# A tokenizer, attention and mixture-of-experts tower in float32: the second MLP product from seven products of quarters, with small work moved between engines

## Chip, cores and metric

The kernel runs on one core of one Trainium2 chip, in float32 throughout. The metric is the device time of one execution in microseconds. Where a profile is read, it is one profiled execution. Engines are named as the profile names them: PE is TensorE (PEld its weight loads), DVE is VectorE, ACT is ScalarE, POOL is GpSimd, SP is SyncE, which issues most DMAs.

## The reference, cut to what matters

The input x is (4, 64, 512, 64): 4 x 4096 = 16384 tokens of 256 features come out.

```python
h = tok(x)                       # patches of 16 at stride 8, real FFT, product with W: (tokens, 256)
x = layernorm(h)
a = layernorm(x) * g1 + b1
q, k, v = a @ Wq.T + bq, a @ Wk.T + bk, a @ Wv.T + bv
mem_t = decay * mem_(t-1) + k_t * v_t          # a scan along the tokens
x = x + q * mem
a = layernorm(x) * g2 + b2
x = x + relu(a @ W1.T + b1) @ W2.T + b2        # W1: 256 to 1024, W2: 1024 to 256, the second MLP product
h = h + x
t = layernorm(h)
p = softmax(t @ router.T)                      # 8 experts; two largest kept, scaled to sum 1
out = h + t + sum over the two experts e of p_e * (gelu(t @ w1[e]) @ w2[e] + b2[e])
```

## The kernel before, in words

**Blocks and stages.** The tokens are worked on in 32 blocks of 512 (`Block`, four tiles of 128 rows). The loop over the blocks (lines 973 to 1047) is a pipeline of three: in one turn `new` (block i) is embedded, normalised and taken through q, k, v and the scan; `mid` (i-1) goes through the MLP; `old` (i-2) is stored, its experts are chosen, and its rows are scattered to a table in DRAM, `xbuf`, sorted by expert. A `Tile` is 256 rows of one expert, read back from `xbuf`; four tiles per block go through the expert's two products in slots between the other work (`expert_step`, line 939, through `slot`, line 959), and their results are added to `out` by indirect DMAs of POOL (line 853).

**Order.** On PE, DVE, ACT and SP the order of the instructions is the order in which the program emits them (`manual_schedule`, line 970); each engine works through its queue in order. Only POOL's order is chosen by the scheduler. A turn of the loop emits: `embed` with an expert slot after it; eight `mlp_in` (first MLP product, line 482 applies ReLU on ACT into `aT`) with a second slot among them; the `logits` of `old` (line 553); `retention(0)`, `choose` of `old`, `retention(1)` (q, k, v products, line 298; ACT makes `ks`, DVE `kv`, the scan and `ret`); `place` (line 619) and `take` (line 696); a third slot; `mlp_out(0)`; `residual` (PE transposes of `ret`, line 451); a fourth slot; `mlp_out(1)`.

**What the change touches.**
- `mlp_out` (line 484): for two tiles of 128 rows at a time, 2 x 8 products of 128x128 by 128x256 into one `tm` buffer of PSUM; DVE adds it to `h` (line 499) and takes the mean and variance of the rows (lines 223, 224). After the second call the factor `rstd` is made on POOL (lines 243, 248), and DVE writes `tok`, the normalised rows.
- PSUM has four buffers `mm`, three `tm`, and a single one named `sm` (line 93). `sm` holds the logits, and then the counts of the placement.
- `embed` (to line 396): at its end DVE writes `zz` and `z`, two normalisations of `h`, four instructions each (line 252), with `rstd` from POOL. `zz` goes by ACT copies and a transposing DMA (line 286) to `hT`, which the q, k, v products read; `z` is needed at `residual`.
- `differences` (line 315): nine DVE operations on the next block's input.
- `choose` (line 565): thirteen small DVE operations on the logits, and one power on POOL. `place` (line 619): two products into `sm`, then DVE operations that read it (lines 629, 630) and give the row addresses; `weights` (line 599).
- `scatter` (line 642): POOL writes the rows of `old` to `xbuf`, two indirect DMAs for each of four tiles.
- `take` (line 696): small DVE operations on one partition that work out, for the next four tiles, the rows and the expert; SP reads that `table` in front of the tiles' loads (lines 775, 779).
- `Tile.sums` (line 838): DVE works out the weights of a tile's rows (`tile_share`, lines 842, 845) and multiplies the tile's results with them.

## Time and profile before

| | us |
|---|---|
| median of 3 runs | 2169.24 (2166.68 to 2170.31) |
| the profiled execution, its own time | 2168.11 |
| its span on the core | 2166.3 |
| a steady period (q, k, v products of one block to those of the next) | 63.4 |
| of this, DVE busy (993.30 to 1056.70) | 50.4 |
| of this, ACT busy | 25.9 |
| of this, POOL busy | 27.8 |

The groups of the page give one row for each line, engine and shape; each float32 matmul of the program stands there as two instructions.

```profile
L492 PE MATMUL tm<-w_sb,aT 128*128 128x256 f32 x2048 | 453.5, 380 | 1.7 <-DVE h L499 1.7
L492 PEld LDWEIGHTS tm<-w_sb,aT 128*128 128x128 f32 x2048 | 389.3, 190 | 55.1 <-DVE h L499 2.1
L597 POOL TENSOR_TENSOR ex<-euler,second 128x4 f32<-128x4 f32 x32 | 34.6, 1080 | 236.7 <-DVE second L589 236.7
```

The number after the bar is the time in which at least one of the group ran, then the mean of one in ns, then the idle time of the engine just before. A mean of 380 ns with 2048 instructions in 453.5 us tells that they overlap: the time that one costs is that from start to start. The last row shows a group whose engine waits for another one most of the time.

### The profile page before, as it was taken

Reading aid. Unit: us, or ns where it says so; the run is one execution under the profiler, and the core shown is the slowest. Engines: PE = TensorE matmul, PEld = TensorE weight load, DVE = VectorE, ACT = ScalarE, POOL = GpSimd, SP = SyncE. Lnnn points to the kernel's source line nnn. Section 1 sums busy time; section 2 is a strip of 40 time slices with the busy share of each in tenths; the row PEclk is TensorE's granted clock in tenths of the full one; section 3 lists DMA queues with packets and bytes.
Section 4 is the critical chain, followed back from the end, with each engine's and each line's share of the span. In section 5 each row is a group of like instructions: output and inputs, shape, how many; then the busy total and the mean of one; then the engine's idle time right before and its main releaser. Section 6 shows DMA issues by size and latency. Waiting matters only on the chain.

```text
span 2166.3 us, 28918 instructions
## 1 busy us (share of the span) xinstructions
PE 2142.5 (99%) x8548; PEld 1545.3 (71%) x8548; DVE 1646.8 (76%) x5150; ACT 833.4 (38%) x1329; POOL 874.0 (40%) x760
## 2 busy tenths in 40 slices
PE   8999999999999999999999999999999999998999
PEld 6666666677776667776667777666777766676776
DVE  6678877787878778787777877877787787767454
ACT  1222333443334444333444433344443334442543
POOL 0022233444444344444334444443444444355444
PEclk9999999999999999999999999999999999999999
DMA  3032255765756675665777556577666657678753
GB/s 138 20 99 77 77 130 127 162 124 128 155 130 148 152 163 117 135 154 127 150 152 156 123 138 146 131 151 154 135 137 145 143 132 153 136 175 216 114 69 44
DMA packets 425389, 284.95 MB, mean 132 GB/s; under 512 B 355216, under 2 KB 391056, under 8 KB 421136
## 3 DMA queue, kind: packets, MB, share of 16 engines
q1 hardware_dynamic: 374304, 210.21, 41.1%
q0 software_dynamic: 49632, 67.39, 17.8%
q10 hardware_dynamic: 1296, 5.52, 0.8%
q8 instruction: 67, 1.10, 0.2%
q14 instruction: 90, 0.74, 0.1%
HBM read 118.36 MB, written 88.39 MB: 95 GB/s over the span
## 4 chain that ended last, share of the span: by engine, by line
PE 96%; DVE 2%; issue 1%; DMA 0%; another core or an unknown queue 0%; ACT 0%; POOL 0%; DVEq 0%; SPq 0%; POOLq 0%; ACTq 0%
PE mm L298 35%; PE tm L492 20%; PE tm L353 13%; PE mm L813 10%; PE tm L830 10%; PE sm L557 2%; PE tm L905 1%; PE tm L451 1%; PE mm L888 1%; PE mm L131 1%; PE mm L265 1%; PE sm L624 0%; PE sm L204 0%; DVE ks L426 0%
## 5 line engine op out<-in xcount | busy, mean ns | idle before, releaser
L853 POOL DMA_INDIRECT out<-y,xg x262 | 429.0, 1637 | 463.4 <-DVE y L849 221.0
L298 PE MATMUL mm<-hT,w_sb 128*128 128x512 f32 x1024 | 453.1, 595 | 3.5 <-issue 2.7
L492 PE MATMUL tm<-w_sb,aT 128*128 128x256 f32 x2048 | 453.5, 380 | 1.7 <-DVE h L499 1.7
L492 PEld LDWEIGHTS tm<-w_sb,aT 128*128 128x128 f32 x2048 | 389.3, 190 | 55.1 <-DVE h L499 2.1
L298 PEld LDWEIGHTS mm<-hT,w_sb 128*128 128x128 f32 x1024 | 195.1, 191 | 221.8 <-issue 207.4
L647 POOL DMA_INDIRECT xbuf<-row,to x248 | 243.5, 982 | 258.7 <-DVE full L708 182.3
L298 PE MATMUL mm<-hT,wqkv_sb 128*128 128x512 f32 x768 | 338.7, 597 | 0.0
L353 PE MATMUL tm<-wu,xv 128*128 128x256 f32 x1280 | 284.3, 381 | 0.0
L353 PEld LDWEIGHTS tm<-wu,xv 128*128 128x128 f32 x1280 | 244.4, 191 | 32.7
L821 ACT ACTIVATE ge<-mm,w 128x256 f32<-128x256 f32 x262 | 109.4, 470 | 404.9 <-issue 363.5
L298 PEld LDWEIGHTS mm<-hT,wqkv_sb 128*128 128x128 f32 x768 | 144.3, 191 | 169.0 <-issue 155.3
L813 PE MATMUL mm<-xT,w 128*128 128x256 f32 x1048 | 250.3, 382 | 1.4 <-DVE tile_share L842 1.4
L830 PE MATMUL tm<-w,ge 128*128 128x256 f32 x1048 | 247.7, 379 | 0.9 <-ACT ge L821 0.9
L482 ACT ACTIVATE aT<-mm,vec 128x512 f32<-128x512 f32 x256 | 172.4, 683 | 187.7 <-PE mm L298 187.0
L813 PEld LDWEIGHTS mm<-xT,w 128*128 128x128 f32 x1048 | 195.0, 191 | 38.1 <-issue 15.6
L830 PEld LDWEIGHTS tm<-w,ge 128*128 128x128 f32 x1048 | 199.4, 190 | 31.0 <-issue 3.3
L806 ACT COPY xT<-xh 128x512 uint16<-128x512 uint16 x262 | 181.6, 763 | 20.3 <-DMA xh<-xbuf 20.2
L243 POOL TENSOR_SCALAR rstd<-mv 128x4 f32<-128x4 f32 x62 | 41.6, 672 | 316.7 <-DVE mv L224 314.8
L278 ACT COPY planes<-zz 128x1024 uint16<-128x1024 uint16 x100 | 99.6, 1043 | 167.4 <-issue 86.8
L847 DVE TENSOR_TENSOR y<-tm,w 128x512 f32<-128x512 f32 x131 | 90.6, 692 | 70.8 <-PE tm L830 70.8
L416 ACT ACTIVATE ks<-mm,vec 128x512 f32<-128x512 f32 x64 | 44.0, 687 | 236.1 <-PE mm L298 236.1
L597 POOL TENSOR_TENSOR ex<-euler,second 128x4 f32<-128x4 f32 x32 | 34.6, 1080 | 236.7 <-DVE second L589 236.7
(155 smaller groups left out, 2443.0 us busy)
## 6 DMA issues: line engine op xcount, KB each, us to landing
w<-in_wex SPq DMA_DIRECT2D x113, 641.5 KB
xb<-in_x SPq DMA_DIRECT2D x32, 1040.0 KB
out<-h SPq DMA_DIRECT2D x31, 512.0 KB
bank<-in_wex ACTq DMA_DIRECT2D x8, 641.5 KB
out<-y,xg POOLq DMA_INDIRECT x262
xbuf<-row,to POOLq DMA_INDIRECT x248
xh<-xbuf SPq DMA_TRANSPOSE x131
xg<-xbuf SPq DMA_DIRECT2D x131, 4.0 KB
```

What stands on the lines that cost most here:

```text
L278: nc.scalar.copy(planes[:, :, i * D : (i + 1) * D], half)
L298: nc.tensor.matmul(ps, lhsT=w[:, k, ts(m, P)], rhs=rhs[:, k, :], start=k == 0, stop=k == KD - 1)
L353: nc.tensor.matmul(ps[:, n, :], lhsT=xv[:, i, j, :], rhs=wu[:, i, j, :], start=j == 0, stop=j == J - 1)
L482: nc.scalar.activation(self.aT[:, m, :], ps, AF.Relu, bias=vec[:, MB1 + m : MB1 + m + 1])
L492: last_product[0] = nc.tensor.matmul(ps[:, i, :], lhsT=self.aT[:, k, ts(u * 2 + i, P)], rhs=w2_sb[:, k, :], start=k == 0, stop=k == KH - 1,)
L647: write = nc.gpsimd.indirect_dma_start(out=xbuf, out_offset=bass.IndirectOffsetOnAxis(ap=self.to[:, c, t : t + 1], axis=0), in_=self.row[: ...
L806: nc.scalar.copy(halves[:, :, :, 1 - i], self.xh[:, i * KD : (i + 1) * KD, :])
L813: nc.tensor.matmul(ps[:, m, :], lhsT=self.w[:, k * D + m * P : k * D + (m + 1) * P], rhs=self.xT[:, k, :], start=k == 0, stop=k == KD - 1,)
L821: nc.scalar.activation(self.ge[:, m, :], ps[:, m, :], AF.Gelu, bias=self.w[:, 5 * D + m : 5 * D + m + 1])
L830: last_product[0] = nc.tensor.matmul(ps[:, c, :], lhsT=self.ge[:, k, ts(c, P)], rhs=w[:, (2 + k) * D : (3 + k) * D], start=k == 0, stop=k ...
L847: nc.vector.tensor_tensor(y, ps, w[:, 4 * D : 5 * D].unsqueeze(1).to_broadcast([P, 2, D]), ALU.add)
L853: add = nc.gpsimd.indirect_dma_start(out=out, out_offset=bass.IndirectOffsetOnAxis(ap=self.xg[:, c, NUMBER - D : NUMBER - D + 1], axis=0), ...
```

## The change

Of `take` the diff shows the lines after the change alone; before, each was on DVE (lines 715 to 744).

**Second MLP product.** `aT` is cut into four quarters (features by rows), `W2` into four (features by outputs), and the product of 2 x 2 quarters is made from seven products of quarters instead of eight, in Winograd's form of Strassen's scheme. `combine_weights` makes the three further combinations of weights once. `combine1` makes three combinations of `aT` on DVE, ahead of the q, k, v products of `new`; `combine2` the fourth, after `mlp_out(0)`. Each product of quarters is eight matmuls of 128x128 by 128x128. They stand in three calls: `mlp_out(0)`, one product, into the buffer `sm`; `mlp_out(1)`, two, into a `tm`, right after it; `mlp_out(2)`, four, where the second call was, two into the same `sm` and two into a `tm`. A copy on ACT and eight adds on DVE bring the seven into `h`.

**Choice of experts.** `choose` is emitted ahead of `retention(0)`, not between the two halves.

**`z`.** It is written by ACT (`result1`), four instructions between the two `ks` of the retention, with a small operation `less` on DVE after the first half of the retention.

**Weights of a tile's rows.** `tile_share` is worked out by POOL when the tile is turned, two tiles ahead, in three operations; in the last blocks by DVE as before. **The table** of `take` is worked out by POOL, from `base` on, in 17 operations that POOL has, except for the last blocks. **Differences**: one operation goes ahead of `zz`, the other eight stay. Some buffers are fewer (`xh` four instead of six). The scatters of the second and third tile now follow `mlp_out(0)` and `mlp_out(1)`.

```diff
@@ weights of the second product @@
-    w2_sb = const.tile([P, KH, D], F32)
-    nc.sync.dma_start(out=w2_sb, in_=w2.rearrange("(k p) d -> p k d", p=P))
+    w2_sb = const.tile([P, 7, KQ, P], F32)
+    w2_raw = w2.rearrange("(r k p) (c d) -> p r c k d", p=P, k=KQ, d=P)
+    for i, (r, c) in {B11: (0, 0), B21: (1, 0), B22: (1, 1), T1: (0, 1)}.items():
+        nc.sync.dma_start(out=w2_sb[:, i], in_=w2_raw[:, r, c])
+    def combine_weights():
+        nc.vector.tensor_tensor(w2_sb[:, T3], w2_sb[:, B22], w2_sb[:, T1], ALU.subtract)
+        nc.vector.tensor_tensor(w2_sb[:, T1], w2_sb[:, T1], w2_sb[:, B11], ALU.subtract)
+        nc.vector.tensor_tensor(w2_sb[:, T2], w2_sb[:, B22], w2_sb[:, T1], ALU.subtract)
+        nc.vector.tensor_tensor(w2_sb[:, T4], w2_sb[:, B21], w2_sb[:, T2], ALU.subtract)
...
@@ Block.differences, Block.embed @@
-        def differences(self, xb):
+        def differences(self, xb, part):
+            if part:
+                self.rest()
+                return
...
-            self.z = one.tile([P, TT, D], F32, name="z")
             self.zz = one.tile([P, TT, D], F32, name="zz")
             norm.apply(self.zz, self.h, 1)
-            norm.apply(self.z, self.h, 0)
+            self.norm1 = norm
+        def result1(self):
+            mean, rstd = self.norm1.mv[:, :, 0], self.norm1.rstd[:, 0, :]
+            less = small.tile([P, TT], F32, name="less")
+            self.z = one.tile([P, TT, D], F32, name="z")
+            nc.vector.scalar_tensor_tensor(less, mean, -1.0, rstd, ALU.mult, ALU.mult)
+            for t in range(TT):
+                nc.scalar.activation(
+                    self.z[:, t, :],
+                    self.h[:, t, :],
+                    AF.Identity,
+                    bias=less[:, t : t + 1],
+                    scale=rstd[:, t : t + 1],
+                )
...
@@ Block.combine1, combine2, mlp_out @@
             ps = feature_mm(w1_sb, self.hT, m)
             nc.scalar.activation(self.aT[:, m, :], ps, AF.Relu, bias=vec[:, MB1 + m : MB1 + m + 1])
 
+        def combine1(self):
+            self.A11, self.A12 = [self.aT[:, i * KQ : (i + 1) * KQ, : BLK // 2] for i in range(2)]
+            self.A21, self.A22 = [self.aT[:, i * KQ : (i + 1) * KQ, BLK // 2 :] for i in range(2)]
+            shape = [P, KQ, BLK // 2]
+            self.S1 = one.tile(shape, F32, name="tok")
+            self.S2 = one.tile(shape, F32, name="tokT")
+            self.S3 = self.A21
+            nc.vector.tensor_tensor(self.S1, self.A21, self.A22, ALU.add)
+            nc.vector.tensor_tensor(self.S2, self.S1, self.A11, ALU.subtract)
+            nc.vector.tensor_tensor(self.S3, self.A11, self.A21, ALU.subtract)
+        def combine2(self, place):
+            self.S4 = one.tile([P, KQ, BLK // 2], F32, name=place)
+            nc.vector.tensor_tensor(self.S4, self.A12, self.S2, ALU.subtract)
         def mlp_out(self, u, between=None):
+            def product(to, a, b):
+                for i in range(2):
+                    for k in range(KQ):
+                        last_product[0] = nc.tensor.matmul(
+                            to[:, i, :],
+                            lhsT=a[:, k, ts(i, P)],
+                            rhs=w2_sb[:, b, k, :],
+                            start=k == 0,
+                            stop=k == KQ - 1,
+                        )
+            def add(to, what):
+                nc.vector.tensor_tensor(to, to, what, ALU.add)
+            h = self.h.rearrange("p (a i) (c d) -> p a c i d", i=2, d=P)
+            U = self.aT[:, 0, : BLK // 2].rearrange("p (i d) -> p i d", d=P)
             if u == 0:
-                self.norm = Norm()
-            ps = p_tm.tile([P, 2, D], F32, name="tm")
-            for i in range(2):
-                if i and between:
+                self.ps = p_sm.tile([P, 2, 2, P], F32, name="sm")
+                product(self.ps[:, 0], self.A11, B11)
+                nc.scalar.copy(U, self.ps[:, 0])
+                add(h[:, 0, 0], U)
+                return
+            if u == 1:
+                ps = p_tm.tile([P, 2, 2, P], F32, name="tm")
+                product(ps[:, 0], self.A12, B21)
+                if between:
                     between()
-                for k in range(KH):
-                    last_product[0] = nc.tensor.matmul(
-                        ps[:, i, :],
-                        lhsT=self.aT[:, k, ts(u * 2 + i, P)],
-                        rhs=w2_sb[:, k, :],
-                        start=k == 0,
-                        stop=k == KH - 1,
-                    )
-            nc.vector.tensor_tensor(self.h[:, ts(u, 2), :], ps, self.h[:, ts(u, 2), :], ALU.add)
-            for i in range(2):
-                self.norm.stats(self.h, u * 2 + i)
-            if u == U - 1:
-                self.norm.factors_here() if self.i >= NS - 1 else self.norm.factors()
-                self.tok = one.tile([P, TT, D], F32, name="tok")
-                self.norm.apply(self.tok, self.h)
-                if self.i == NS:
-                    nc.vector.tensor_tensor(self.h, self.h, self.tok, ALU.add)
-                    return
-                mean, rstd = self.norm.mv[:, :, 0], self.norm.rstd[:, 0, :]
-                self.by = small.tile([P, 2, TT], F32, name="by")
-                nc.vector.tensor_scalar(self.by[:, 0, :], rstd, 1.0, None, ALU.add)
-                nc.vector.scalar_tensor_tensor(self.by[:, 1, :], mean, -1.0, rstd, ALU.mult, ALU.mult)
+                product(ps[:, 1], self.A22, T4)
+                add(h[:, :, 0], ps)
+                return
+            product(self.ps[:, 1], self.S2, T2)
+            product(self.ps[:, 0], self.S1, T1)
+            add(U, self.ps[:, 1])
+            add(h[:, 0, 1], U)
+            add(h[:, :, 1], self.ps[:, 0].unsqueeze(1).to_broadcast([P, 2, 2, P]))
+            if between:
+                between()
+            ps = p_tm.tile([P, 2, 2, P], F32, name="tm")
+            product(ps[:, 0], self.S3, T3)
+            product(ps[:, 1], self.S4, B22)
+            add(U, ps[:, 0])
+            add(h[:, 1], U.unsqueeze(1).to_broadcast([P, 2, 2, P]))
+            add(h[:, 0, 1], ps[:, 1])
+            self.norm = Norm()
+            for t in (2, 3, 0, 1):
+                self.norm.stats(self.h, t)
+            self.norm.factors_here() if self.i >= NS - 1 else self.norm.factors()
+            self.tok = one.tile([P, TT, D], F32, name="tok")
+            self.norm.apply(self.tok, self.h)
+            if self.i == NS:
+                nc.vector.tensor_tensor(self.h, self.h, self.tok, ALU.add)
+                return
+            mean, rstd = self.norm.mv[:, :, 0], self.norm.rstd[:, 0, :]
+            self.by = small.tile([P, 2, TT], F32, name="by")
+            nc.vector.tensor_scalar(self.by[:, 0, :], rstd, 1.0, None, ALU.add)
+            nc.vector.scalar_tensor_tensor(self.by[:, 1, :], mean, -1.0, rstd, ALU.mult, ALU.mult)
 
...
@@ take @@
+        engine = nc.vector if block.i >= SOON else nc.gpsimd
         base = small.tile([1, E + 1], F32, name="base")
+        engine.tensor_tensor(base[:, :E], taken, upto[:, :E], ALU.subtract)
+        engine.tensor_scalar(base[:, E:], upto[:, E:], -1.0, None, ALU.mult)
+        engine.tensor_scalar(base, base, float(S), None, ALU.mult)
+        engine.tensor_tensor(base, base, first[0:1, :], ALU.add)
         step = small.tile([1, E], F32, name="step")
+        engine.tensor_tensor(step, base[:, 1:], base[:, :E], ALU.subtract)
         shape = [1, k, E]
+        past = one.tile([1, 2, KMAX, E], F32, name="past")[:, :, :k, :]
+        engine.tensor_tensor(
+            past[:, 0],
             tile_f[:, :k].unsqueeze(2).to_broadcast(shape),
             upto[:, 1:].unsqueeze(1).to_broadcast(shape),
+            ALU.subtract,
         )
+        engine.tensor_scalar(past[:, 0], past[:, 0], 0.0, None, ALU.is_ge)
+        engine.tensor_tensor(past[:, 1], past[:, 0], step.unsqueeze(1).to_broadcast(shape), ALU.mult)
+        for half in (E // 2, E // 4):
+            engine.tensor_tensor(
+                past[..., :half], past[..., :half], past[..., half : 2 * half], ALU.add
+            )
+        table_f = one.tile([1, 2, KMAX], F32, name="table_f")[:, :, :k]
+        engine.tensor_tensor(table_f, past[:, :, :, 0], past[:, :, :, 1], ALU.add)
+        engine.tensor_tensor(table_f[:, 1, :], tile_s[:, :k], table_f[:, 1, :], ALU.add)
         table = four.tile([1, 3, KMAX], I32, name="table")[:, :, :k]
+        engine.tensor_scalar(table[:, 0, :], table_f[:, 0, :], float(P), float((E - 1) * P), ALU.mult, ALU.min)
+        engine.tensor_scalar(table[:, 1, :], table_f[:, 1, :], base[:, 0:1], None, ALU.add)
         if block.i >= NS - 1:
+            engine.tensor_scalar(table[:, 2, :], table_f[:, 0, :], float(E - 1), None, ALU.min)
         if n < NS:
+            engine.tensor_scalar(upto, upto, float(k), None, ALU.min)
+            engine.tensor_tensor(taken, taken, upto[:, 1:], ALU.add)
+            engine.tensor_tensor(taken, taken, upto[:, :E], ALU.subtract)
         for t in range(k):
...
@@ Tile @@
-            self.xh = six.tile([P, 2 * KD, S], U16, name="xh")
+            self.xh = four.tile([P, 2 * KD, S], U16, name="xh")
...
         def turn(self):
+            self.share = four.tile([P, 2], F32, name="tile_share")
+            self.tag = None
+            if self.block.i < NS - 1:
+                self.tag = self.w[:, 5 * D + KD : 5 * D + KD + 1]
+                self.shares(nc.gpsimd)
...
+        def shares(self, engine):
+            share, given = self.share, self.xg.bitcast(F32)
+            engine.tensor_scalar(share, given[:, :, FIRST - D], self.tag, None, ALU.is_equal)
+            engine.tensor_tensor(share, share, given[:, :, DIFF - D], ALU.mult)
+            engine.tensor_tensor(share, share, given[:, :, SECOND - D], ALU.add)
         def sums(self):
             w, ps = self.w, self.ps
-            share = small.tile([P, 2], F32, name="tile_share")
-            tag = w[:, 5 * D + KD : 5 * D + KD + 1]
-            nc.vector.scalar_tensor_tensor(
-                share, self.xg.bitcast(F32)[:, :, FIRST - D], tag, self.xg.bitcast(F32)[:, :, DIFF - D], ALU.is_equal, ALU.mult
-            )
-            nc.vector.tensor_tensor(share, share, self.xg.bitcast(F32)[:, :, SECOND - D], ALU.add)
+            if self.tag is None:
+                self.tag = w[:, 5 * D + KD : 5 * D + KD + 1]
+                self.shares(nc.vector)
+            share = self.share
...
@@ the loop over blocks @@
             next(embed)
             if mid:
                 mid.sum_up()
+            blocks[i + 1].differences(xs.pop(i + 1), 0)
             next(embed, None)
             slot(known, load=False)
             if old:
@@ -1007,27 +1111,34 @@
                 if m == KH // 2 and old:
                     old.store()
                 if m == KH - 3:
-                    blocks[i + 1].differences(xs.pop(i + 1))
+                    blocks[i + 1].differences(None, 1)
                     new.features1()
             if i == NS - 1:
                 slot(known)
             if old:
                 for t in range(TT):
                     old.logits(t)
+            if old:
+                old.choose()
+            if mid:
+                mid.combine1()
             for m in range(KD):
                 new.retention(m)
-                if old and m == 0:
-                    old.choose()
+                if m == 0:
+                    new.result1()
             if old:
                 take(old.i + 1, old, old.place(at_once=False))
                 old.scatter(1)
             if i + 2 < NB:
                 xs[i + 2] = load_x(i + 2)
             slot(known)
+            if mid:
+                mid.mlp_out(0)
             if old:
                 old.scatter(2, last_product[0])
             if mid:
-                mid.mlp_out(0)
+                mid.combine2("kv")
+                mid.mlp_out(1)
             if old:
                 old.scatter(3, last_product[0])
             new.residual()
@@ -1039,12 +1150,13 @@
                 advance("load", 2)
             if i == 0:
                 fold(w1_sb.unsqueeze(1), G2, B2, MB1)
+                combine_weights()
             else:
                 new.split2()
             if at["enter"]:
                 advance("load", at["enter"] + AHEAD - 1)
             if mid:
-                mid.mlp_out(1)
+                mid.mlp_out(2)
 
...
@@ after the loop @@
+        last.combine1()
+        last.combine2("kv")
         expert_step()
-        last.mlp_out(0, expert_step)
+        last.mlp_out(0)
+        last.mlp_out(1, expert_step)
         expert_step()
-        last.mlp_out(1, expert_step)
+        last.mlp_out(2, expert_step)
```

## Prediction

> **What bounds the kernel now.** I read the page from the top: busy times first, then the chain that ended last.

> ```profile
> PE 2142.5 (99%) x8548; PEld 1545.3 (71%) x8548; DVE 1646.8 (76%) x5150; ACT 833.4 (38%) x1329; POOL 874.0 (40%) x760
> PE 96%; DVE 2%; issue 1%; DMA 0%; another core or an unknown queue 0%; ACT 0%; POOL 0%; DVEq 0%; SPq 0%; POOLq 0%; ACTq 0%
> ```

> TensorE (PE) is the bound with almost no gaps: less work on it is worth its full time, and a new wait on it costs its full time too. So I went on to the timeline of one steady block, first PE.

> ```profile
> 992.93 10.55 PE L298 MATMUL mm<-hT,wqkv_sb 128*128 128x512 f32 x24
> 1003.32 0.53 PE L624 MATMUL sm<-both,rc 128*128 128x32 f32 x4
> 1003.68 1.97 PE L813 MATMUL mm<-xT,w 128*128 128x256 f32 x8
> 1005.49 1.89 PE L830 MATMUL tm<-w,ge 128*128 128x256 f32 x8
> 1007.22 7.07 PE L492 MATMUL tm<-w_sb,aT 128*128 128x256 f32 x32
> 1014.12 1.04 PE L451 MATMUL tm<-ident,ret 128*128 128x128 f32 x8
> ```

> Columns: start, duration, engine, line. The same q, k, v products start again at 1056.34, so a period is 63.4 us, without a gap. The second MLP product (L492) is two such runs of 6.9 us, start to next start. PE comes to the first one 14.3 us after the q, k, v products begin (992.93 to 1007.22). Now DVE and ACT in that stretch.

> ```profile
> 996.73 0.75 DVE L418 SCALAR_TENSOR_TENSOR kv<-mm,vec,ks 128x512 f32<-128x512 f32 x1 [3.50 <-PE mm L298]
> ...
> 999.79 0.18 DVE L579 COPY lg<-sm 128x32 f32<-128x32 f32 x1
> ...
> 1002.58 0.74 DVE L418 SCALAR_TENSOR_TENSOR kv<-mm,vec,ks 128x512 f32<-128x512 f32 x1
> ...
> 1006.72 0.19 DVE L630 TENSOR_TENSOR before<-sm,before 128x32 f32<-128x32 f32 x1
> ```

> ```profile
> 1000.08 0.69 ACT L416 ACTIVATE ks<-mm,vec 128x512 f32<-128x512 f32 x1 [4.46 <-PE mm L298]
> ```

> DVE has 3.5 us free before its first `kv`; the choice runs between the two halves (2.8 us); L630 is the last reader of the one `sm` buffer in PSUM, which today nobody on PE wants until the next block's logits. Last, GpSimd.

> ```profile
> 1025.56 1.61 POOL L853 DMA_INDIRECT out<-y,xg  x1 [2.68 <-DVE y L849]
> 1027.47 1.57 POOL L853 DMA_INDIRECT out<-y,xg  x1 [0.30 <-DVE mv L224]
> 1029.11 0.23 POOL L243 TENSOR_SCALAR rstd<-mv 128x4 f32<-128x4 f32 x1
> 1029.43 1.04 POOL L248 TENSOR_TENSOR rstd<-rstd,mhalf 128x4 f32<-128x4 f32 x1
> ...
> 1037.16 1.11 POOL L243 TENSOR_SCALAR rstd<-mv 128x4 f32<-128x4 f32 x1 [6.58 <-DVE mv L224]
> ```

> POOL is 40% busy, yet its queue is on a path of DVE: the factor `rstd` of `tok` came only after two adds to `out`, and DVE waited 3.05 us for it.

> [...] the same 128x4 operation takes 0.23 us at 1029.11 but 1.11 us at 1037.16, while DVE adds two SBUF tensors. [...] The trace shows a mean clock of 0.95 in 1965 to 2030, where PE was busy 58.7 of 65 us.

> **The change part by part.**

> *Products.* Per block 32 matmuls of 256 columns become 56 of 128; each f32 matmul is two recorded instructions. Start to start, 64 took 13.8 us: 216 ns each. The transposes (128 columns) took 0.88 us for 8 (1014.12 to 1015.00), 110 ns; the logits, 8 columns each, 16 in 1.71 us, 107 ns[...]. If loads hide: 112 x 110 ns = 12.3 us, a gain of 1.5 us per block, 48 us over 32. Below: 107 ns, 59 us. [...] I take 110[...].

> *DVE.* Per block it gains three 1024-element adds (combine1, 1.22 us each from L463), a fourth (combine2), and in the output five narrow adds of 0.42 and three of 0.69 in place of two of 0.69: in all +7.7 us. It loses `z` (1.6), the shares (4 x 0.37 = 1.5) and the table (2.5): net about +2 on 50.4 of 63.4 us. By sum DVE isn't the bound.

> *Order, the place that decides.* `mlp_out(0)` now writes `sm`, so PE must wait for the last reader of the placement's `sm`. In the changed order that reader stands behind: logits result 0.15, choice 2.8, combine1 3.7, first half of the retention 3.1 (996.73 to 999.8), `less` 0.15, then ACT's four `z` (2.06, from the four of L518) ahead of the second `ks` on ACT's queue (0.7, with 0.1 of hand-over), second half on DVE 3.05 (1002.58 to 1005.63), placement up to L630 1.3. Sum 17.1 us against PE's 14.3: a stall of 2.8 us per block. Without the `z` ahead of `ks` it would be 14.3, just hidden. Queued behind it on PE is everything, so it is paid in full. 26 blocks (those with an expert tile in that slot) x 2.8 = 73 us. Three early blocks have no tile there (133.07 to 143.81 is 10.7 us): 6.4 each, 19 us, and [...] about 3.3 more each (0.05 of the 65 us above), 10.

> *GpSimd.* Per block 17 small table operations and 12 for four tiles' shares. A price from both sides: 0.2 + 0.1 us (uncontended L243 and its gap) to 0.6 [...]; I take 0.3. From the start of q, k, v: placement and weights of rows done at 17.1 + 1.4 = 18.5, first scatter 0.8 later (as 1008.31 to 1009.12). In POOL's new order there stand before `tok`'s `rstd`: 8 scatters x 1.27 = 10.2, 4 adds to `out` x 1.93 = 7.7, 17 x 0.3 = 5.1, itself 1.5: ready at 43.8, against 37.5 today (1030.47). DVE waits there in order. From `tok` to the end of the `hT` copies took 26.2 us today (1030.51 to 1056.68), 2.6 of it waits; less `z` (1.3) and two shares (0.75): 21.5, plus 2 for the second `rstd`, now behind shares that wait for their tile's rows by DMA. Sum 67.3, less 0.35 (PE starts on the first half of `hT`): a loop of 67.0 us. PE's own is 63.4 - 1.5 + 2.8 = 64.7. The longer counts: 67.0.

> *What costs nothing.* `w2` in four DMAs and combine_weights (4 x 0.69 once): before 92 us, where the first L492 stands; with no cover 3 us once. Fewer `xh` buffers: each is read by ACT more than one slot before its next load; uncovered, a slot of 3.5 us. The tile table on POOL: SP waits for it in front of a tile's load and the next transposes, but the load waits for the scatters anyway, which stand behind the table on POOL. Split differences: same operations.

> *The tail.* Two blocks: 2.0 us more on DVE after each last product and 1.4 of combine1 uncovered, +6, less 3 of products: +3.

> *Sum*, on the profiled execution's own 2168.1 us (span 2166.3; the median shown, 2169.2, is 1.1 higher): 26 x (67.0 - 63.4) = +94; four early blocks -6 + 19 + 10 = +23; tail +3. 2288 us.

> **Rivals.**
> A, only the stall at `sm`, POOL's queue hidden: 26 x (64.7 - 63.4) = +34, +23, +3: 2228. For: POOL is 40% busy. Against: its four `out` adds and eight scatters already fill it up to `tok`.
> B, my forecast, both: 2288; with 0.45 per POOL operation 26 x 2.5 more, 2353.
> C, it ends faster: `sm` is free when PE comes, because the retention's second half isn't held by `z` (2.8 of the 17.1), and POOL keeps up. Then 32 x 1.5 comes off, early stalls of 3.6 x 3 stay and the tail adds 6: 2137. It decides from a chain under 14.3 + 1.5 = 15.8 us. Against: each term is measured, and ACT works in order.
> D, the weight load isn't hidden at 128 columns: [...]
> A change within 0.2% (about what a measurement here can tell from none) needs the stall to equal the gain by accident.

> **How the numbers follow.** B 0.55, A 0.23, D 0.1, C 0.09, no change 0.03. Faster 0.09, same 0.03, slower 0.88. The range takes in A with half its stall gone (26 x 1.4 less, 2192) and B with dear POOL operations and some of D: 2195 to 2370.

> **What would show it.** Right: PE idle of about 3 us per block in front of the first product into `sm`, released by DVE; `tok` on DVE waiting over 5 us for POOL's `rstd`; new products at about 110 ns start to start. Wrong: no gap at `sm` (then C), [...] or gaps at `sm` alone (A).

## The result, and the profile after

| | before | after |
|---|---|---|
| median of 4 runs each, us | 2168.21 | 2297.49 (2292.87 to 2306.3) |
| ratio (95% interval) | | 1.060 (1.0567 to 1.0634) |
| profiled execution, its time and its span | 2168.1; 2166.3 | 2306.3; 2304.5 |
| steady period, mean of 25 | 63.4 | 67.2 (67.0 without the first of them) |
| first four periods | 51.5, 52.2, 57.9, 64.3 | 58.1, 62.4, 67.6, 72.3 |
| time at half clock on PE | 23.2 | 139.4 |

A period is counted from the start of one placement's products to that of the next. The profile records the clock granted to PE; in the traces of both kernels it is full or half, and the last row adds up the records at half. The 138 us between the two spans lie so: 2.8 before the first placement (143.5 to 146.3), 26.5 in the first three periods (161.6 to 188.1), 94 in 25 steady ones (25 x 3.76, the fourth of the list being their first) and 14.7 from the last of them to the end. The profiled execution of the changed kernel is the longest of its four, 9 us above their median.

The page of the changed kernel, its busy times and its chain that ended last:

```profile
PE 2161.0 (94%) x10084; PEld 1598.4 (69%) x10084; DVE 1747.1 (76%) x4801; ACT 896.6 (39%) x1489; POOL 1112.9 (48%) x1559
PE 6%; DVE 1%; POOL 0%; DMA 0%; issue 0%; ACT 0%; DVEq 0%; POOLq 0%
```

PE was 99% busy and is 94% busy: 143 us without work in place of 24. The chain can't be used here, since it was followed back through about 7% of the span only. So the waits come next, first those of PE, then those of DVE (waits in us, how many, the longest):

```profile
PE sm L543 <- DVE before L714: 90.2, 29, 6.4
PE mm L312 <- ACT aT L518: 10.7, 9, 2.2
```

```profile
DVE tok L266 <- POOL rstd L262: 115.5, 30, 8.4
DVE kv L454 <- ACT ks L452: 86.8, 31, 2.8
DVE zz L266 <- POOL rstd L262: 81.1, 32, 3.6
```

One wait makes up most of PE's: the first product into `sm` (L543), released by the reader of the placement's counts (L714, which was L630). Its place in a steady block, on PE:

```profile
996.92 10.54 PE L312 MATMUL mm<-hT,wqkv_sb 128*128 128x512 f32 x24
1007.29 0.53 PE L708 MATMUL sm<-both,rc 128*128 128x32 f32 x4
...
1009.47 1.89 PE L928 MATMUL tm<-w,ge 128*128 128x256 f32 x8
1014.22 3.75 PE L543 MATMUL sm<-w_sb,aT 128*128 128x128 f32 x16 [2.87 <-DVE before L714]
1017.76 4.91 PE L543 MATMUL tm<-w_sb,aT 128*128 128x128 f32 x32
1022.51 1.04 PE L487 MATMUL tm<-ident,ret 128*128 128x128 f32 x8
```

On DVE, and then on ACT, at the same time:

```profile
995.98 1.45 DVE L306 COPY hT<-turned 128x512 uint16<-128x512 uint16 x4
997.33 0.18 DVE L663 COPY lg<-sm 128x32 f32<-128x32 f32 x1
...
1006.76 0.16 DVE L414 SCALAR_TENSOR_TENSOR less<-mv,rstd 128x4 f32<-128x4 f32 x1
1009.72 0.75 DVE L454 SCALAR_TENSOR_TENSOR kv<-mm,vec,ks 128x512 f32<-128x512 f32 x1 [2.80 <-ACT ks L452]
...
1013.88 0.19 DVE L714 TENSOR_TENSOR before<-sm,before 128x32 f32<-128x32 f32 x1
```

```profile
1007.03 2.07 ACT L416 ACTIVATE z<-h,less,rstd 128x256 f32<-128x256 f32 x4 [7.44 <-POOL tile_share L939]
1009.01 0.67 ACT L452 ACTIVATE ks<-mm,vec 128x512 f32<-128x512 f32 x1
```

Before, the second `kv` followed the first half without a wait; now DVE waits 2.8 us for a `ks` that stands behind four `z`. DVE also comes from its copy of `hT` straight to the logits' result (997.33), without idle time; this will matter for the second theory below. And PE loses more than its 2.87 us: the 16 products after the gap take 3.54 us, start to start, and not 1.79. In stretches around the gap the granted clock (third column from the end; the first is the stretch, then its length and the busy times of PE, PEld, DVE, ACT, POOL) tells why:

```profile
1013.00:1014.00 1.00, 0.00 (x0) 0.00 (x0) 0.78 (x5) 0.00 (x0) 0.00 (x0) 0.70 0.00 0
1014.00:1017.50 3.50, 3.28 (x15) 3.31 (x16) 3.09 (x18) 0.00 (x0) 1.11 (x1) 0.50 0.02 5
1017.50:1024.00 6.50, 6.50 (x46) 6.45 (x45) 3.14 (x6) 1.67 (x3) 5.70 (x11) 0.79 0.17 61
```

Last GpSimd, from the first scatter to `rstd`:

```profile
1016.28 1.11 POOL L731 DMA_INDIRECT xbuf<-row,to  x1 [8.04 <-DVE full L792]
...
1018.94 1.19 POOL L803 TENSOR_SCALAR base<-upto 1x1 f32<-1x1 f32 x1
1020.11 0.23 POOL L810 TENSOR_TENSOR past<-tile_f,upto 1x32 f32<-1x32 f32 x1
...
1039.09 1.05 POOL L262 TENSOR_TENSOR rstd<-rstd,mhalf 128x4 f32<-128x4 f32 x1
```

`rstd` is ready 43.2 us after the q, k, v products began (1040.14 less 996.92), 37.5 before the change.

### The profile page after: what moved, and what is told of

It reads as the page before. It is cut to its first block, busy times and chain, and to the rows that moved or that the text cites. A ratio compares the mean times of both kernels' runs of the same rounds, so it can differ in the third digit from the quotient of the medians.

```text
span 2304.5 us, 32783 instructions
## 1 busy us (share of the span) xinstructions
PE 2161.0 (94%) x10084; PEld 1598.4 (69%) x10084; DVE 1747.1 (76%) x4801; ACT 896.6 (39%) x1489; POOL 1112.9 (48%) x1559
## 3 DMA queue, kind: packets, MB, share of 16 engines
q1 hardware_dynamic: 375376, 210.21, 38.9%
## 5 line engine op out<-in xcount | busy, mean ns | idle before, releaser
L312 PE MATMUL mm<-hT,w_sb 128*128 128x512 f32 x1024 | 454.2, 594 | 11.0 <-ACT aT L518 10.7
L731 POOL DMA_INDIRECT xbuf<-row,to x248 | 258.5, 1042 | 327.6 <-DVE full L792 252.7
L938 POOL TENSOR_SCALAR tile_share<-xg,w 128x2 f32<-128x2 f32 x113 | 70.8, 627 | 328.6 <-DMA xg<-xbuf 328.6
L518 ACT ACTIVATE aT<-mm,vec 128x512 f32<-128x512 f32 x256 | 167.7, 688 | 86.5 <-PE mm L312 86.3
L543 PE MATMUL tm<-w_sb,aT 128*128 128x128 f32 x1536 | 193.6, 285 | 0.0
L543 PEld LDWEIGHTS tm<-w_sb,aT 128*128 128x128 f32 x1536 | 189.8, 203 | 0.1
L543 PE MATMUL sm<-w_sb,aT 128*128 128x128 f32 x512 | 92.2, 354 | 90.2 <-DVE before L714 90.2
L416 ACT ACTIVATE z<-h,less,rstd 128x256 f32<-128x256 f32 x128 | 66.4, 589 | 233.1 <-DVE less L414 196.1
L543 PEld LDWEIGHTS sm<-w_sb,aT 128*128 128x128 f32 x512 | 85.9, 261 | 101.1 <-issue 101.0
```

What stands on the lines that cost most here:

```text
L312: nc.tensor.matmul(ps, lhsT=w[:, k, ts(m, P)], rhs=rhs[:, k, :], start=k == 0, stop=k == KD - 1)
L518: nc.scalar.activation(self.aT[:, m, :], ps, AF.Relu, bias=vec[:, MB1 + m : MB1 + m + 1])
L543: last_product[0] = nc.tensor.matmul(to[:, i, :], lhsT=a[:, k, ts(i, P)], rhs=w2_sb[:, b, k, :], start=k == 0, stop=k == KQ - 1,)
L731: write = nc.gpsimd.indirect_dma_start(out=xbuf, out_offset=bass.IndirectOffsetOnAxis(ap=self.to[:, c, t : t + 1], axis=0), in_=self.row[: ...
L938: engine.tensor_scalar(share, given[:, :, FIRST - D], self.tag, None, ALU.is_equal)
```

## The experiments

Two theories. **W**: the late chain on DVE and ACT, its wait at `sm` and the half clock after it make the period; GpSimd's queue lies below. **Q**: the loop over GpSimd's queue (scatters, table, `rstd`, `tok`, `hT`) would hold the period at 66 to 67 us by itself. The late chain stands at the head of that loop too, since the first scatter waits for the placement. The rows give the median, the ratio to the kernel before, measured together with it, the mean steady period, the sum of the first three periods (161.6 before, 188.1 after), and PE's time at half clock.

| kernel | us | ratio (95%) | period | first 3 | half clock |
|---|---|---|---|---|---|
| two calls swapped | 2316.6 | 1.068 (1.067, 1.070) | 68.1 | 182.6 | 138.9 |
| `z` after the retention | 2196.8 | 1.013 (1.011, 1.015) | 63.7 | 180.6 | 53.6 |
| table and shares back on DVE | 2272.2 | 1.048 (1.046, 1.050) | 66.5 | 179.2 | 114.8 |
| swap, table and shares back | 2290.6 | 1.057 (1.055, 1.058) | 67.3 | 173.5 | 132.6 |
| `z` after, table and shares back | 2181.4 | 1.006 (1.004, 1.008) | 63.4 | 171.7 | 43.1 |
| `z` after, shares back | 2236.9 | 1.032 (1.029, 1.034) | 65.6 | 174.1 | 145.7 |
| new product alone | 2225.4 | 1.026 (1.023, 1.029) | 64.9 | 175.8 | 56.9 |
| moves alone | 2182.2 | 1.007 (1.005, 1.010) | 63.5 | 170.5 | 26.7 |
| `z` after, table back | 2169.7 | 1.000 (0.999, 1.001) | 63.0 | 172.4 | 51.8 |
| `z`, table, shares; third slot first | 2201.8 | 1.015 (1.014, 1.017) | 64.0 | 172.2 | 52.6 |
| the same, counts in `mm` | 2195.9 | 1.012 (1.010, 1.013) | 64.0 | 166.1 | 38.9 |
| the same, shares on POOL | 2179.9 | 1.005 (1.004, 1.007) | 63.4 | 166.9 | 35.2 |

**The two calls swapped** (the products into `tm` first, which need no `sm`):

```diff
-                mid.mlp_out(0)
+                mid.mlp_out(1)
...
-                mid.mlp_out(1)
+                mid.mlp_out(0)
```

> The two products into tm (second call) go ahead of the one into sm (first call), in the loop alone. PE then has 3.6 us of work while sm is still being read. Theory W (the wait at sm and the halved clock after it are what makes the period 67.2 us; GpSimd's queue lies below): the 2.9 us gap and most of the half clock go, the period falls to about 62.5, the three early blocks keep some 2.8 us of their gap: about 2155 us. Theory Q (the loop through GpSimd's queue holds the period at 66 to 67 by itself): the gap only moves to the q, k, v products, which wait for hT: about 2270 us or more.

Measured: 2316.6, slower still: W's 2155 is a miss, and Q's 2270 or more is the nearer. The gap left `sm`, and PE waits as long elsewhere:

```profile
PE mm L312 <- ACT aT L518: 89.8, 26, 4.5
PE sm L543 <- DVE before L714: 7.9, 3, 2.8
```

DVE's waits for `tok`'s `rstd` grew from 115.5 to 181.0 us. The new gap isn't in front of the q, k, v products, as Q had it, but among the first MLP products: these wait for an `mm` buffer that ACT's `aT` frees behind its copies of `zz`, and DVE writes `zz` after a `tok` that waited 6.3 us for `rstd` in the block at 1001.30. A wait that keeps its size when PE's order is changed isn't made by that buffer: PE runs ahead of something that is late itself, on DVE and ACT. Whether `z` or `rstd` makes it late, this kernel doesn't tell.

**`z` after the retention**, so behind the second `ks` on ACT:

```diff
             for m in range(KD):
                 new.retention(m)
-                if m == 0:
-                    new.result1()
+            new.result1()
```

> The four z instructions go behind the second ks on ACT. The chain in front of sm shortens by 2.8 us to 14.3, the same as PE's way. Theory W: the gap at sm shrinks to under 0.5 us in the steady blocks and to 3.6 in the three early ones, the half clock goes with it: about 2165 us. Theory Q: the loop through GpSimd begins with the same chain and shortens by 2.8 to 64.2 us: about 2220 us. If z is not what holds the second half of the retention, nothing changes: 2297.

Measured: 2196.8, 101 us less than the changed kernel, from a move of five instructions, and between the 2165 of W and the 2220 of Q; the three waits left at `sm` are those of the early blocks. PE's waits:

```profile
PE mm L312 <- ACT aT L518: 16.3, 25, 2.4
PE sm L543 <- DVE before L714: 10.0, 3, 3.4
PE mm L312 <- DVE hT L306: 6.1, 25, 1.8
```

DVE still waits 4.7 us per block for `tok`'s `rstd` (140.9 in 30), with all the table's and the shares' operations on GpSimd, and the period is 63.7. So that queue alone doesn't make 66 us; but this isn't a test of W against Q, since `z` stood at the head of both. What holds 63.7 looks like the loop, near the 64.2 of Q: in 25 blocks PE waits for DVE's `hT` in front of the q, k, v products, by 0.2 us in most.

**Table and shares back on DVE**:

```diff
-        engine = nc.vector if block.i >= SOON else nc.gpsimd
+        engine = nc.vector
...
-            if self.block.i < NS - 1:
+            if False:
```

> The table and the weights of a tile's rows go back to DVE, all else as changed. GpSimd's queue loses 29 small operations per block and its waits for the tiles' rows; the chain in front of sm stays. Theory W: the gap at sm and the clock stay, so the time stays near 2297 (2285 to 2310). Theory Q: the queue no longer holds the period, which falls to PE's 64.7 and some clock: 2230 to 2250 us.

Measured: 2272.2, only 25 us less, between the two ranges and nearer to that of W. PE's waits and DVE's:

```profile
PE sm L543 <- DVE before L714: 88.1, 29, 6.4
```

```profile
DVE kv L454 <- ACT ks L452: 86.8, 31, 2.8
DVE zz L266 <- POOL rstd L262: 50.8, 32, 2.1
DVE tok L266 <- POOL rstd L262: 44.7, 30, 1.5
```

The wait at `sm` is unchanged while the one for `tok`'s `rstd` fell from 115.5 to 44.7 us. And PE no longer waits for DVE's `hT` in front of the q, k, v products, as it does in the changed kernel (2.6 us in 12 waits). So this is close to rival A of the prediction, PE's own path, at 66.5 us and not 64.7 per period; DVE is some 4 us busier here than rival A had it, and PE's waits for `h` and `y`, 7.5 us in all, are new with it. W makes 3.1 of the 3.8 us by which the period grew, and GpSimd's work adds 0.7 on top.

**Both edits, swap and GpSimd's work back.**

> Both edits: the products swapped as in the first, and GpSimd's new work back on DVE. Both theories: neither the gap at sm nor the queue is left, the period falls to PE's own 62.1 to 63: 2140 to 2165 us. If it stays above 2200, DVE itself, now about 4 us per block busier, has become the bound.

Measured: 2290.6, a miss for both theories. DVE as the bound, the third reading, doesn't fit either, since DVE still waits 86.8 us for `ks`. PE now waits for the transposes' `tm`, which late `y` (the third slot's result, behind the placement and the table on DVE's queue) holds:

```profile
PE tm L487 <- DVE y L949: 86.7, 26, 3.8
```

86.7 us, against 88.1 at `sm` and 89.8 at `mm`: nearly the same size at three places. Here `rstd` is hardly late (44.6 us in 30 waits), so what is left to be late is the chain with `z`.

**`z` after, and GpSimd's work back**:

> z behind the second ks, and the table and the weights of a tile's rows back on DVE. The chain in front of sm is 14.3 us, and nothing of the new small work is in GpSimd's queue. Both the wait and the queue are then out of the way, and the period is PE's own, 62.1 to 62.7 us; the three early blocks keep about 3.5 us at sm and some half clock: 2140 to 2160 us, under the kernel before. If DVE, some 4 us busier per block, has become the bound, 2170 to 2210.

Measured: 2181.4, above the 2160 of W and Q and in the range given for DVE as the bound. PE has two small waits a block (0.48 for `tm` behind the first addition to `h`, 0.34 behind `y`). In the two periods from 900 to 1026 DVE waits for nobody but the two `rstd`, its whole list of waits being:

```profile
DVE zz L266 <- POOL rstd L262: 3.1, 2, 1.6
DVE tok L266 <- POOL rstd L262: 3.0, 2, 1.5
```

and in one period (columns as above):

```profile
940.88:1004.29 63.41, 62.59 (x303) 45.88 (x302) 57.07 (x176) 27.86 (x46) 28.34 (x24) 1.00 0.67 143
```

57.07 busy and 3.05 of waits for `rstd` leave 3.3 us of small steps between 176 instructions: DVE in order has become the bound, at 90% busy. It never waits for PE in that stretch.

**`z` after, only the shares back.**

> z behind the second ks, and only the weights of a tile's rows back on DVE; the table stays on GpSimd. If it is the shares' wait for their rows by DMA in GpSimd's queue (279 us in all with z behind ks) that holds the factors, the time falls to that with everything back, 2140 to 2165. If it is the 17 table operations between the scatters, it stays near 2195.

Measured: 2236.9, and inconclusive on the shares: the scheduler, which chooses POOL's order alone, put the table's operations in a row and two adds to `out` ahead of most scatters, and `tok` waits 4.3 us per block again (130.1 in 30), and PE 1.4 us for `hT` (35.1 in 25): the loop of Q, as the longer path. It shows two other things. The seventeen table operations in a row took 1046.69 to 1051.75, 0.30 us each. And the clock: the logits, 8 columns each, and then 1.37 us of idle time, are followed by half clock in 25 of the 26 steady blocks, whose 24 instructions of the q, k, v products take 11.94 to 13.60 us and not 10.55:

```profile
1024.08 1.85 PE L641 MATMUL sm<-rw_sb,tokT 128*128 128x8 f32 x16
1027.30 6.88 PE L312 MATMUL mm<-hT,wqkv_sb 128*128 128x512 f32 x12 [1.37 <-DVE hT L306]
```

**New product alone** (choice between the halves, `z`, table and shares on DVE as before the change):

```diff
+            norm.apply(self.z, self.h, 0)
...
                 new.retention(m)
+                if old and m == 0:
+                    old.choose()
```

> Seven products alone: choice between the halves, z, the table and the weights of a tile's rows all on DVE as before. DVE has all of the 7.7 us more per block: 58 of 62 us. PE's way to sm is 14.3 us, and the chain is 0.15 + 3.7 + 3.1 + 2.8 + 3.05 + 1.3 = 14.1: no gap at sm by this. If the chain is what counts: 2140 to 2170. If DVE at 94% can't keep up: 2180 to 2240, with gaps on PE released by DVE.

Measured: 2225.4, as the second forecast had it, with a period of 64.9 and DVE busy for 113.3 us of the 126 from 900 to 1026. Alone, the product loses 2.6%. PE's waits, the largest:

```profile
PE mm L312 <- DVE hT L306: 24.5, 25, 1.3
PE tm L918 <- DVE h L542: 12.6, 26, 0.5
```

**Moves alone**: the old product, in the places of the new one (its first half where the first two calls stand; `combine1` and `combine2` empty); everything else as changed.

> All moves (z on ACT ahead of the second ks, table and weights on GpSimd, choice first, products' places), but the second MLP product as before, in eight products of quarters, in tm buffers. sm isn't written by it, and combine1 and combine2 are not there: the chain is 3.7 us shorter and nobody on PE waits for its end. Both theories: PE's own 63.4 us, 2160 to 2180 us. If GpSimd's queue alone made the loss: 2230 and more.

Measured: 2182.2, 2 us above the range, and a period of 63.5. Two periods of it:

```profile
900.00:1027.00 127.00, 127.00 (x506) 91.41 (x506) 91.75 (x270) 55.31 (x90) 68.33 (x107) 1.00 0.67 142
```

PE is without a gap, although DVE waits for `ks` (86.8 us, as in the changed kernel) and 5.1 us per block for `tok`'s `rstd`. Where nothing on PE wants `sm` early and DVE is at 72%, neither the early `z` nor GpSimd's work costs anything in the steady state; its span is 13.7 us longer by the first three periods (8.9), by what stands ahead of them (3.1), and by 25 x 0.06.

**`z` after, table back, shares left on GpSimd**:

> The changed kernel with z written after the whole retention and only the table of take back on DVE; the weights of the tiles' rows stay on GpSimd. Theory W (the late chain at sm and the half clock it brings make the period, GpSimd's queue lies below): with z out of the way the chain at sm is short enough whatever GpSimd does, so this is like z alone, a period of 63.3 to 63.7 us and 2190 to 2200 us. Theory Q (17 table operations ahead of rstd are what GpSimd's queue costs, the shares little): DVE waits under 2 us per block for rstd, the period is about 63.0 and the time 2165 to 2178, less than z with everything back on DVE, since DVE has 1.5 us less per block.

Measured: 2169.7, the time of before, and as Q had it: W held that the table on GpSimd costs nothing once `z` is out of the way, and it costs 27 us (2196.8 less 2169.7), since `tok` now waits 1.5 us for `rstd` and not 4.7. So Q's mechanism is real, at a fraction of the size it was given. Two periods:

```profile
900.00:1025.60 125.60, 124.57 (x596) 90.94 (x595) 109.17 (x323) 55.62 (x92) 61.85 (x70) 1.00 0.66 143
```

PE has 62.3 us of work in 62.8 and 63.4 before: the new product saves 1.1 us per period. That shows in 25 periods, 11.3 us less by their mean of 62.99, and is given back in the first three (10.8) and in the tail (6.8). The profiled execution, at 2174.8, is the longest of its 13.

**The third slot ahead of `take`**, on the kernel with `z` after and GpSimd's work back; then **the counts of the placement in `mm`**:

```diff
-                take(old.i + 1, old, old.place(at_once=False))
+                writes = old.place(at_once=False)
+            slot(known)
+            if old:
+                take(old.i + 1, old, writes)
...
-            slot(known)
```

```diff
-            ps = p_sm.tile([P, 2, TT, E], F32, name="sm")
+            ps = p_mm.tile([P, 2, TT, E], F32, name="mm")
```

> z after the retention, table and weights of rows on DVE, and the third expert slot emitted between the placement and take, so that the tile's results leave DVE's queue some 3.6 us earlier and the tm buffer they hold is free when PE wants it for the second call of the second product. If waits of PE for tm (8.8 us there) and for h (12.5 us) are what keeps the period at 63.4, it goes to 62.3 to 62.8 and the time to 2155 to 2168. If DVE at 90% is the bound by sum, nothing changes: 2178 to 2185.

> The kernel before this one with the counts of the placement in an mm buffer of PSUM in place of sm, so that nothing but the logits precedes the first product in sm. The three early blocks' gaps in front of sm (3.4 us each, 10.0 in all) go, with the clock they cost: 8 to 14 us under the kernel with the slot first. If the gap only moves to the next wait for DVE there (mm, tm), less than 4 us under it.

Measured: 2201.8 and 2195.9, two misses. The wait for `y` went, and that for `h` grew in its place, to 1.5 us a block:

```profile
967.84 1.97 PE L928 MATMUL tm<-w,ge 128*128 128x256 f32 x8 [1.54 <-DVE h L552]
```

With DVE the bound, an earlier instruction makes another later. The counts in `mm` took the early gaps away (the first three periods fell by 6.1), about 6 us and not 8 to 14.

**The same with the shares on GpSimd**:

> As the kernel before this one (z after the retention, table on DVE, third slot ahead of take, counts in mm), with the weights of the tiles' rows on GpSimd. If DVE's sum is the bound, 1.5 us less per block on DVE shows: 2135 to 2150. If GpSimd's waits for a tile's rows by DMA hold up rstd and so tok, it is slower than the kernel before this one: above 2165, with DVE waiting over 100 us in all for rstd.

Measured: 2179.9, and neither expectation: the time lies in the second's range, its mechanism isn't there, for the waits for `tok`'s `rstd` are 45.6 us in all. Against the kernel before this one it is 16 us less, and the period is 0.55 us shorter for 1.5 us less on DVE: a bound by DVE's sum holds for about a third of that, and then DVE waits for PE (67.5 us for the experts' products before `y`, 37.2 in the kernel before). So the shares on GpSimd don't hold `rstd` up once the table is gone. The kernel with `z` after and the table back, with the counts in `mm` too, wasn't tried; no kernel that ran beats the one before.

## Why the prediction was right, and where its working was off

The forecast was 2288 us, 0.4% under the median, and the sign and the place are shown. By its steps:

- *Products.* At full clock 16 instructions take 1.79 us, start to start (1029.44 to 1031.22 in the kernel with `z` after and GpSimd's work back): 112 ns, against 110. A weight load of these products is recorded with 192 ns (the median for L543 in the changed kernel), so loads overlap with the products and with each other, and rival D is out. The saving was put at 1.5 us per block and is 1.1.
- *The stall at* `sm`. The chain was put at 17.1 us against PE's 14.3. In the block shown it is 17.3 (996.92 to 1014.22) against 14.4 (to 1011.36): 2.9, and 2.7 on average over 26 blocks (90.2 less 3 x 6.3). Its cause is shown by the one edit that takes `z` from ahead of `ks`.
- *The clock.* Here a term was mis-sized. The working charged half clock to three early blocks, 10 us in all, and nothing to the steady ones. It comes in 19 stretches over the 26 steady blocks. What it costs: the kernel with `z` after and the table back has as many PE instructions and 38.6 us less PE busy time for 87.6 us less at half clock, 0.44 us lost for each. The changed kernel has about 75 us at half clock in its 26 steady blocks: by this 1.3 us per period, 33 in all, and with the early blocks and the tail 51 us more than before (116 x 0.44). 18 of the 19 follow a gap of 2.5 to 2.9 us at `sm`. That a gap of this length leaves the clock alone was the author's assumption, which no trace of before showed, and it was the failing step. What the traces show of these stretches stands in the last section.
- *The path of PE* by these terms is 63.4 - 1.1 + 2.7 + 1.3 = 66.3 us, where the working had 64.7; the kernel with GpSimd's work back has 66.5. With 0.4 of waits for `aT` and 0.1 for `hT` the changed kernel's sum is 66.8, against 67.0 without the first of the 25 periods.
- *The loop over GpSimd.* `rstd` was to be ready at 43.8 and is at 43.3 on average; from `tok` to the end of the `hT` copies it was to be 23.5 and is 24.3 with its waits. So the loop, put at 67.0, is met, by two small errors of opposite sign. It also does hold the period in most blocks: in 17 of the 26 the q, k, v products start 0.36 to 0.77 us after the last instruction of the logits, as DVE's `hT` releases them, and not 0.11; with GpSimd's work back it is 0.11 in every one. That "the longer counts" was right. But it isn't the cause of the whole: with GpSimd's work back 66.5 is left. The two paths nearly tie, with `z` at the head of both; GpSimd's work adds 0.7 us per period, 25 us in all, and the working put 60 on it (2288 less 2228). The price of an operation, put at 0.3 us, is 0.35 on average for the table. In the steady blocks eleven of the 425 operations took over 0.9 us, and each ran while DVE added two SBUF tensors (L534), as the one of 1.19 at 1018.94; most of the others took 0.19 to 0.64, as the one of 0.23 at 1020.11. The sign "`tok` waits over 5 us" wasn't met: 3.9.
- *Rival A* was therefore priced too low (2228), by the clock and by the smaller saving. As run it is 2272. This error didn't reach the forecast, because the longer path was taken, and that came out right. That the shorter one was 1.8 us wrong and still lay below is luck.
- *Early blocks.* +23 was the forecast; the first three periods are 26.5 longer and what stands ahead of them 2.8. The three stalls are 6.2 to 6.4 us as said (6.4).
- *The tail.* +3 forecast, +14.7 measured. 6.8 stays in the kernel with `z` after and the table back, and so belongs to the product's adds or to the moves; of the rest a stall at `sm` is about 3. The remainder wasn't taken apart.
- *DVE by sum.* "Net about +2 on 50.4, not the bound" is right for the changed kernel (52.8 on the mean of the 25 periods). But it is near enough that with table, shares and the new adds, 57.1, DVE in order is the bound at 63.4. The working didn't look for that.

## What to carry to other kernels

Before work is put on an engine's queue, ask what the next instruction there releases: four `z` of 0.5 us in front of one `ks` cost 100 us of 2300. A gap on the busiest engine is priced with the clock that follows it: here 1.3 us per period on top of the gap's 2.7. When a gap moves with its size unchanged from buffer to buffer, look upstream: the buffer is only where the lateness is noticed. And when one edit shortens two paths at once, as moving `z` did, it can't tell which of the two was the longer; take away what only one of them has.
